# The first layer norm of a four-layer graph kernel: a fixed order on three engines, a centring product kept in PSUM, and the listing of pairs cut into pieces

## The chip, the cores and the metric

The kernel runs on one core of a Trainium2 chip. The metric is the device time of one execution in microseconds. The kernel before took 2083.43 us, the median of three runs (2079.95 to 2089.01). One more execution was profiled; it took 2082.92 us.

## The reference

Eight graphs of 2048 nodes with 64 features go through four layers. Each layer is a pre-norm residual block, and they share one adjacency matrix:

```python
h = jnp.maximum(_layernorm(x, axis=-1), 0.0)
x = x + layer(h)      # four different graph layers
```

with

```python
def _layernorm(x, axis=-1, eps=1e-5):
    m = jnp.mean(x, axis=axis, keepdims=True)
    v = jnp.var(x, axis=axis, keepdims=True)
    return (x - m) / jnp.sqrt(v + eps)
```

The first layer computes `industry`, the row-normalised adjacency matrix times `h @ W_ind`, and an attention between nodes and 64 hyperedges, whose membership matrix `H` (2048 x 64, zeros and ones) is given. Only the norm ahead of the first layer, the product with `W_ind` and the preparation of `H` are touched here.

## The kernel before, in words

The features lie transposed, two graphs on the 128 partitions: `xT[p]` is a block of 128 x 2048 for each of four pairs of graphs. The first norm treats each block in two halves of 1024 columns, so there are eight halves.

For one half the steps are: load `x` in two DMAs of 128 x 512; multiply it on TensorE by `avg`, a matrix that holds 1/64 in each graph's 64 x 64 block, which leaves the mean in PSUM (`mean`, L744); subtract on DVE (VectorE) into `xc` in SBUF (L745); square on ACT (ScalarE, L746); multiply by `avg` again (`var`, L751); logarithm and exponential on ACT to get the reciprocal root (L752, L753); one DVE instruction for `max(xc, 0) * q` into `hn` (L754). Then eight products of 128 x 128 with `W_ind` give `py` (L902), in two PSUM tiles of four products each. ACT copies each `py` rounded into `Y[0]` (L904), and DVE writes the rounding difference into `Y[1]` (L905). After that comes the industry stage: for each of four columns of 512 nodes, 16 tiles of the adjacency matrix are streamed in eight transfers `at` (L932, issued by POOL into a ring of six buffers), and products `acc` (L940) sum both parts of `Y` over them. Between these products lie the members' units (`ph`, L982, and the ACT and DVE work behind it), and DVE sums the `at` tiles into `ds` (L945).

The listing of pairs, `pairs`, runs after the first block: it loads `M` and `MT` (the membership matrix and its transpose), turns them to zeros and ones on DVE (L846, L848), ranks the pairs by products with a triangular matrix (`pr`, L857, and `pc`, L861) and copies, adds and multiplies on DVE until `Q` is there (L868). It also reduces `MT` into a flag (`bad`, L878). The weights of layers 0, 1 and 2 are prepared after the second and third block, with small products `pw`, `pwc` and `pwb` on TensorE and many small DMAs on SP.

In this stage a scheduler orders the instructions of each engine when the program is built; it works from its own estimates of when each operand is ready. Some instructions are instead kept in the order of the text: those issued through `kit.mm` while `kit.strict` is on, and those issued through the wrapper `InOrder`. In the first norm of the kernel before, none but the loading of ACT's table are.

[...] The stage's tiles take them all: `mean` two, `var` two of two banks each, and a tag `yy` with two tiles of one bank, which `py`, `pr`, `pc` and the weights' small products take in turn. A tile is used again when its last reader is done.

Of the kernel before, what the change touches and what calls it, by code (L numbers as in the profile page):

```python
# [8 lines left out]
FP = mybir.dt.float32  # L9
FR = mybir.dt.float32r  # L10
AF = mybir.ActivationFunctionType
OP = mybir.AluOpType
# [622 lines left out]
class Kit:  # L635


    def __init__(self, tc, t, pool):
# [8 lines left out]
        for b2 in range(2):  # L647
            nc.vector.memset(self.avg[half(b2), half(b2)], 1.0 / F)
        self.eps = pool.tile([P, 1], FP, name="eps_f")
# [107 lines left out]
    def norm(self, *tiles):  # L757
        for _ in self.norm_steps(*tiles):
            pass


def layer0(kit, hn, x1_dram, open_early, late_tile, between):
# [40 lines left out]
    with ExitStack() as sA:  # L803
# [29 lines left out]
        def pairs(pool, ps):  # L833
# [4 lines left out]
            nc.vector.tensor_copy(slot, tmp)  # L838
            tri = pool.tile([P, P], FP, name="tri")
            nc.gpsimd.iota(tmp[:, 0:P], pattern=[[1, P]], base=0, channel_multiplier=-1)  # L840
            nc.vector.tensor_copy(tri, tmp[:, 0:P])
            nc.vector.tensor_scalar(tri, tri, 0.0, None, op0=OP.is_ge)
            for h in range(2):
                nc.sync.dma_start(out=M[:, :, h, :], in_=t["L0_gnn_H"].rearrange("(t p) e -> p t e", p=P))
            Mf = M.rearrange("p t h e -> p (t h e)")
            nc.vector.tensor_scalar(Mf, Mf, 0.0, None, op0=OP.is_gt)  # L846
            nc.sync.dma_start(out=MT, in_=t["HT"])
            nc.vector.tensor_scalar(MT, MT, 0.0, None, op0=OP.is_gt)  # L848
# [3 lines left out]
            past = pool.tile([P, NT], FP, name="past")  # L852
            for g in range(2):
                pr = ps.tile([P, 8, E], FP, tag="yy", name="pr")
                for k in range(8):
                    i = 8 * g + k
                    mm(pr[:, k, :], MT[:, i * P : (i + 1) * P], tri[0:E, 0:E], start=True, stop=True)  # L857
                nc.vector.tensor_copy(rank[:, 8 * g : 8 * g + 8, :], pr)
            nc.vector.tensor_copy(deg, rank[:, :, E - 1])
            pc = ps.tile([P, NT], FP, tag="yy", name="pc")  # L860
            mm(pc, tri, deg, start=True, stop=True)  # L861
            nc.vector.tensor_copy(past, pc)
            nc.vector.tensor_sub(first, past, deg)

            nc.vector.tensor_tensor(rank, rank, first[:, :, None].to_broadcast([P, NT, E]), op=OP.add)
            nc.vector.tensor_tensor(rank, rank, M[:, :, 0, :], op=OP.mult)
            for h in range(2):
                nc.vector.tensor_scalar(Q[:, :, h, :], rank, -1.0, None, op0=OP.add)  # L868
            nc.vector.tensor_tensor(mid, first, past, op=OP.add)
            nc.vector.tensor_scalar(mid, mid, -0.5, 0.5, op0=OP.mult, op1=OP.add)  # L870
            nc.vector.tensor_scalar(width, deg, 0.5, None, op0=OP.mult)

            lo = pool.tile([P, NT], FP, name="bad_t")
            nc.vector.tensor_reduce(bad[:, 0:1], deg, AX.X, OP.min)
            nc.vector.tensor_scalar(bad[:, 0:1], bad[:, 0:1], 0.5, None, op0=OP.is_lt)
            nc.vector.tensor_scalar(lo, past, SLOTS + 0.5, None, op0=OP.is_gt)
            nc.vector.tensor_reduce(bad[:, 1:2], lo, AX.X, OP.max)
            nc.vector.tensor_reduce(bad[0:E, 2:3], MT, AX.X, OP.max)  # L878
            nc.vector.tensor_scalar(bad[0:E, 2:3], bad[0:E, 2:3], 0.5, None, op0=OP.is_lt)


        with ExitStack() as s1:
            pool = s1.enter_context(tc.tile_pool(name="rank", bufs=1, reuse_waits="tile"))
            sb = s1.enter_context(tc.tile_pool(name="nf_sb", bufs=2, reuse_waits="tile"))
            ps = s1.enter_context(tc.tile_pool(name="nf_ps", bufs=2, space=PSUM, reuse_waits="tile"))
            kit.use_ln_exp()
            for p in range(NP):
                for hf in range(2):
                    s = cols(hf, HN)
                    x = sb.tile([P, HN], FP, tag="x", name="x", bufs=3)  # L890
                    for k in range(2):
                        nc.sync.dma_start(out=x[:, cols(k)], in_=t["xT"][p, :, cols(2 * hf + k)])
                    mean = ps.tile([P, HN], FP, tag="mean", name="mean", bufs=1)
                    var = ps.tile([P, HN], FP, tag="var", name="var")
                    xc = sb.tile([P, HN], FP, tag="xc", name="xc")
                    q = sb.tile([P, HN], FP, tag="q", name="q")
                    kit.norm(hn[p][:, s], x, mean, var, xc, q)
                    for c in (2 * hf, 2 * hf + 1):
                        py = ps.tile([P, 4, P], FP, tag="yy", name="py")
                        for k in range(4):  # L900
                            m = 4 * c + k
                            mm(py[:, k, :], hn[p][:, m * P : (m + 1) * P], W_ind, start=True, stop=True)  # L902
                        yh = Y[0][:, 4 * c : 4 * c + 4, p, :]
                        nc.scalar.copy(yh, py)  # L904
                        nc.vector.tensor_tensor(Y[1][:, 4 * c : 4 * c + 4, p, :], py, yh.bitcast(FP), op=OP.subtract)  # L905
                if p == 0:
                    pairs(pool, ps)
                if p == 1:
                    weights(pool, ps)
                    kit.layer1_weights(pool, ps)  # L910
# [1079 lines left out]
```

## Time and profile before

| what | value |
|---|---|
| median of three runs | 2083.43 us |
| the profiled execution | 2082.92 us |
| its span, first to last instruction | 2081.0 us |
| busy share of TensorE, DVE, ACT, POOL | 96%, 58%, 22%, 13% |
| first product of the first norm | 4.03 us from the start of the span |
| first `acc` product of the industry stage | 68.99 us |
| first `acc` product of its second column | 111.64 us |

The first norm with the listing and the weights is therefore a stretch of some 65 us out of 2081. In the profile, PE is TensorE's products and PEld its weight loads; a float32 product has two records. A row of the timeline gives the start, the duration, the engine and line, the operation, the tiles written and read, how many records were merged, and in brackets how long the engine sat idle before it and what ended that. A group's row gives busy time and the mean of one in ns, then the idle time before. Durations of TensorE overlap their neighbours', so the distance between two starts is what one costs.

### The profile page before, as it was taken

To read this page: it belongs to the slowest core of one execution; us is meant where nothing else is said; L and a number is where in the kernel's file an instruction comes from. 1 tells how busy PE (TensorE), PEld (TensorE's weight loads), DVE (VectorE), ACT (ScalarE), POOL (GpSimd) and SP (SyncE) were. 2 spreads that over 40 slices of the span, in tenths; PEclk is the share of its full clock that TensorE was granted. 3 is DMA by queue.
4 is the path that set the end of the run, shared out by engine and by line. 5 is a ranking of instruction groups with operands and counts; after the bars stand their busy time and mean duration, and the time that the engine had idled before them with its cause. 6 is when DMAs were issued, how large, how long until landed. Compare 5 with 4: busy or idle time off the path is not lost.

```text
span 2081.0 us, 23594 instructions
## 1 busy us (share of the span) xinstructions
PE 2005.6 (96%) x9164; PEld 1154.1 (55%) x9164; DVE 1196.8 (58%) x1882; ACT 455.5 (22%) x859; POOL 264.2 (13%) x383
## 2 busy tenths in 40 slices
PE   7999899887999999999999999999999999999997
PEld 4777655533322222227775557765477755577653
DVE  6667478976888888883224653225632156522355
ACT  4321244457112121112121111211111211112100
POOL 0211054422000000000001210002100012100022
PEclk9999899999999999999999999999999999999999
DMA  6666272157111111213200012101022000121000
GB/s 180 195 193 190 67 239 80 43 154 162 46 42 35 49 33 23 60 31 89 66 31 21 25 37 60 58 7 35 18 64 61 26 22 25 37 75 46 8 14 12
DMA packets 84251, 138.16 MB, mean 66 GB/s; under 512 B 32753, under 2 KB 33009, under 8 KB 81457
## 3 DMA queue, kind: packets, MB, share of 16 engines
q1 hardware_dynamic: 65200, 83.86, 13.7%
q0 software_dynamic: 18928, 52.70, 10.2%
q8 instruction: 74, 1.21, 0.2%
q14 instruction: 49, 0.39, 0.1%
HBM read 102.64 MB, written 37.03 MB: 67 GB/s over the span
## 4 chain that ended last, share of the span: by engine, by line
PE 68%; issue 15%; DVE 6%; POOL 4%; DMA 3%; ACT 2%; SPq 0%; POOLq 0%; DVEq 0%; ACTq 0%
PE acc L726 27%; PE o L726 11%; PE u L726 6%; PE dn L726 5%; PE acc L940 3%; PE pgs L1169 2%; PE var L726 2%; PE mean L726 2%; PE py L726 2%; POOL fold L1878 1%; DVE ex L1167 1%; DMA at<-in_adjT 1%; PE ph L726 1%; POOL ot L1879 1%; DMA iv<-ind_dram 1%
## 5 line engine op out<-in xcount | busy, mean ns | idle before, releaser
L726 PE MATMUL acc<-aT,parts 128*128 128x512 f32 x1664 | 456.0, 420 | 0.0
L726 PEld LDWEIGHTS acc<-aT,parts 128*128 128x128 f32 x1664 | 307.8, 188 | 111.8 <-issue 49.4
L1866 DVE TENSOR_TENSOR pr<-u,embf 128x512 f32<-128x512 f32 x256 | 170.7, 688 | 138.8 <-PE u L726 131.9
L1485 DVE SCALAR_TENSOR_TENSOR pt<-R,wd,aT 128x1024 f32<-128x1024 f32 x192 | 236.5, 1279 | 20.4 <-PE dn L726 6.6
L726 PE MATMUL u<-W3f,y 64*128 64x512 f32 x1024 | 241.0, 589 | 0.0
L726 PE MATMUL o<-pt,hS 128*64 128x512 f32 x1024 | 236.4, 599 | 3.0 <-DVE pt L1485 3.0
L726 PEld LDWEIGHTS u<-W3f,y 64*128 64x128 f32 x1024 | 99.2, 187 | 120.6 <-issue 120.6
L726 PEld LDWEIGHTS o<-pt,hS 128*64 128x64 f32 x1024 | 68.0, 136 | 161.4 <-issue 149.9
L940 PE MATMUL acc<-at,Y 128*128 128x512 f32 x512 | 137.0, 413 | 2.4 <-DVE ev L949 2.4
L726 PE MATMUL u<-W3f,v 64*128 64x512 f32 x512 | 138.8, 619 | 0.0
L726 PE MATMUL dn<-pt,vd 128*32 128x512 f32 x1024 | 123.1, 598 | 0.0
L1702 DVE TENSOR_TENSOR yb<-py,cb_f 128x512 f32<-128x512 f32 x32 | 22.1, 691 | 173.7 <-PE py L726 173.7
L1878 POOL TENSOR_TENSOR fold<-fold 128x256 f32<-128x256 f32 x64 | 47.7, 745 | 548.4 <-DVE fold L1877 510.6
L940 PEld LDWEIGHTS acc<-at,Y 128*128 128x128 f32 x512 | 95.8, 195 | 25.7 <-issue 4.3
L726 PE MATMUL acc<-aTl,parts 128*128 128x512 f32 x384 | 103.2, 405 | 0.0
L1870 DVE TENSOR_TENSOR pr<-pr 128x512 f32<-128x512 f32 x128 | 88.1, 688 | 2.2
L1485 DVE SCALAR_TENSOR_TENSOR pt<-R,wd,aTl 128x1024 f32<-128x1024 f32 x64 | 79.8, 1282 | 11.4 <-PE dn L726 8.2
L726 PEld LDWEIGHTS acc<-aTl,parts 128*128 128x128 f32 x384 | 72.2, 188 | 21.5 <-issue 5.7
L1169 PE MATMUL pgs<-mix,S 128*128 128x512 f32 x128 | 69.8, 635 | 13.1 <-POOL mix L1168 12.4
L1852 ACT COPY xs<-px 128x128 f32<-128x128 f32 x64 | 17.1, 267 | 272.7 <-POOL ot L1880 210.3
L1168 POOL TENSOR_TENSOR mix<-ex,wt 128x512 f32<-128x512 f32 x64 | 66.7, 1042 | 76.7 <-DVE ex L1167 66.4
L1770 POOL TENSOR_TENSOR bq<-bq,xp 128x512 f32<-128x512 f32 x16 | 20.5, 1283 | 434.1 <-DVE xp L1768 395.5
(321 smaller groups left out, 2672.8 us busy)
## 6 DMA issues: line engine op xcount, KB each, us to landing
at<-in_adjT POOLq DMA_DIRECT2D x32, 512.0 KB, 4.6
raw<-in_adjT SPq DMA_DIRECT2D x64, 256.0 KB, 3.4
aT<-in_adjT POOLq DMA_DIRECT2D x12, 1024.0 KB, 6.1
xp<-xd SPq DMA_DIRECT2D x45, 256.0 KB, 3.2
R<-r_dram SPq DMA_DIRECT2D x14, 512.0 KB, 3.8
hi_dram<-hi SPq DMA_DIRECT2D x16, 264.0 KB, 2.4
lo_dram<-lo SPq DMA_DIRECT2D x16, 264.0 KB, 3.4
hhi<-hi_dram POOLq DMA_DIRECT2D x16, 264.0 KB, 3.0
```

The lines of the kernel that those rows point to most:

```text
L726: one = self.nc.tensor.matmul(*args, **kw)
L940: mm(acc[p], Y[h][:, m, p, :], at[:, k, :], start=m + h == 0, stop=m == NT - 1 and h == 1)
L1167: nc.vector.scalar_tensor_tensor(ex, mix, 1.0, ex, op0=OP.max, op1=OP.min)
L1168: nc.gpsimd.tensor_tensor(mix, ex, wt[:, k, :, None].to_broadcast([P, B, F]), op=OP.mult)
L1169: return lambda: mm(flat(pg), S[:, k, :], flat(mix), start=k == 0, stop=k == NB - 1)
L1485: nc.vector.scalar_tensor_tensor(pt, R[b2], wd[:, m, b2 : b2 + 1], aT[m][:, s].bitcast(FP), op0=OP.max, op1=OP.mult)
L1702: nc.vector.tensor_tensor(yb, py, bias[:, None, :].to_broadcast([P, 4, P]), op=OP.add)
L1770: nc.gpsimd.tensor_add(bq, bq, xp)
L1866: nc.vector.tensor_tensor(a, u[h], emb[:, i, 8 * w : 8 * w + 8, None].to_broadcast([P, 8, F]), op=OP.mult)
L1870: nc.vector.tensor_add(pr[h], pr[h], a)
L1878: nc.gpsimd.tensor_add(fold[:, :, 0:2, :], fold[:, :, 0:2, :], fold[:, :, 2:4, :])
L1879: nc.gpsimd.tensor_add(ot, fold[:, :, 0, :], fold[:, :, 1, :])
```

## The change

`Kit` gets a matrix `cen`, the identity less `avg`. One product with it leaves `x - mean` in PSUM, where `xc` now stays: the square and the last DVE step read it there, and the subtraction L745 and the SBUF tile are gone. PSUM is dealt out anew: `xc` has two tiles of two banks, `var` has one.

The stage becomes a loop of ten steps over eight halves. In step i the text issues: the loads of half i+2; the variance and scaling of half i-1; the centring and squaring of half i; a piece of the listing; the products with `W_ind` of half i-2 and their two copies. The products go through `kit.mm` with `strict` on, and the ACT and DVE instructions through `InOrder`, so all three engines keep this order. `pairs` is a generator with a `yield` between pieces, and its DVE instructions go through the same wrapper; `MT` is now loaded ahead of `M`, and `M` is compared with zero in a later piece. The weights of layers 0, 1 and 2 are prepared in steps 3, 4 and 5; of these only the issuing place moves.

```diff
+        self.cen = pool.tile([P, P], FP, name="cen_f")
+        nc.vector.tensor_sub(self.cen, self.ident, self.avg)
...
-        def pairs(pool, ps):
+        def pairs(pool, ps, V):
...
+            nc.sync.dma_start(out=MT, in_=t["HT"])
+            for h in range(2):
+                nc.sync.dma_start(out=M[:, :, h, :], in_=t["L0_gnn_H"].rearrange("(t p) e -> p t e", p=P))
+            yield
+            V.tensor_scalar(MT, MT, 0.0, None, op0=OP.is_gt)
+            yield
             for g in range(2):
                 pr = ps.tile([P, 8, E], FP, tag="yy", name="pr")
                 for k in range(8):
                     i = 8 * g + k
-                    mm(pr[:, k, :], MT[:, i * P : (i + 1) * P], tri[0:E, 0:E], start=True, stop=True)
-                nc.vector.tensor_copy(rank[:, 8 * g : 8 * g + 8, :], pr)
-            nc.vector.tensor_copy(deg, rank[:, :, E - 1])
+                    kit.mm(pr[:, k, :], MT[:, i * P : (i + 1) * P], tri[0:E, 0:E], start=True, stop=True)
+                V.tensor_copy(rank[:, 8 * g : 8 * g + 8, :], pr)
+                if g:
+                    V.tensor_copy(deg, rank[:, :, E - 1])
+                yield
             pc = ps.tile([P, NT], FP, tag="yy", name="pc")
+            kit.mm(pc, tri, deg, start=True, stop=True)
+            V.tensor_copy(past, pc)
+            V.tensor_sub(first, past, deg)
+            V.tensor_tensor(rank, rank, first[:, :, None].to_broadcast([P, NT, E]), op=OP.add)
+            yield
+            Mf = M.rearrange("p t h e -> p (t h e)")
+            V.tensor_scalar(Mf, Mf, 0.0, None, op0=OP.is_gt)
+            V.tensor_tensor(rank, rank, M[:, :, 0, :], op=OP.mult)
+            yield
             for h in range(2):
-                nc.vector.tensor_scalar(Q[:, :, h, :], rank, -1.0, None, op0=OP.add)
+                V.tensor_scalar(Q[:, :, h, :], rank, -1.0, None, op0=OP.add)
+            yield
...
+            V.tensor_reduce(bad[:, 1:2], lo, AX.X, OP.max)
+            yield
+            V.tensor_reduce(bad[0:E, 2:3], MT, AX.X, OP.max)
+            V.tensor_scalar(bad[0:E, 2:3], bad[0:E, 2:3], 0.5, None, op0=OP.is_lt)
+            yield
...
-                    kit.norm(hn[p][:, s], x, mean, var, xc, q)
...
+            V, A = InOrder(tc, nc.vector), InOrder(tc, nc.scalar)
...
+            def centred(i):
+                x = xs.pop(i)
+                xc = xcs[i] = ps.tile([P, HN], FP, tag="xc", name="xc")
+                for k in range(2):
+                    kit.mm(xc[:, cols(k)], kit.cen, x[:, cols(k)], start=True, stop=True)
+
+            def squared(i):
+                q = qs[i] = sb.tile([P, HN], FP, tag="q", name="q")
+                A.activation(q, xcs[i], AF.Square)
+
+            def scaled(i):
+                p, hf = halves[i]
+                q = qs.pop(i)
+                var = ps.tile([P, HN], FP, tag="var", name="var", bufs=1)
+                for k in range(2):
+                    kit.mm(var[:, cols(k)], kit.avg, q[:, cols(k)], start=True, stop=True)
+                A.activation(q, var, AF.Ln, bias=kit.eps)
+                A.activation(q, q, AF.Exp, scale=-0.5)
+                V.scalar_tensor_tensor(hn[p][:, cols(hf, HN)], xcs.pop(i), 0.0, q, op0=OP.max, op1=OP.mult)
+
+            def mapped(i):
+                p, hf = halves[i]
+                pys[i] = []
+                for c in (2 * hf, 2 * hf + 1):
+                    py = ps.tile([P, 4, P], FP, tag="yy", name="py")
...
+            def halved(i):
+                p, hf = halves[i]
+                for c, py in pys[i]:
+                    A.copy(Y[0][:, 4 * c : 4 * c + 4, p, :], py)
+                for c, py in pys.pop(i):
+                    ms = slice(4 * c, 4 * c + 4)
+                    V.tensor_tensor(Y[1][:, ms, p, :], py, Y[0][:, ms, p, :].bitcast(FP), op=OP.subtract)
+
+            listed = pairs(pool, ps, V)
+            fetched(0)
+            fetched(1)
+            kit.strict = True
+            for i in range(len(halves) + 2):
+                if i + 2 < len(halves):
+                    fetched(i + 2)
+                if 0 < i <= len(halves):
+                    scaled(i - 1)
+                if i < len(halves):
+                    centred(i)
+                    squared(i)
+                next(listed, None)
+                if i > 1:
+                    mapped(i - 2)
+                    halved(i - 2)
+                if i == 3:
                     weights(pool, ps)
+                if i == 4:
                     kit.layer1_weights(pool, ps)
+                if i == 5:
                     kit.layer2_weights(pool, ps)
+            kit.strict = False
```

## The prediction

> **What bounds the kernel now.** I read the page first (engines, then the chain that ended last), then busy time by stretches, TensorE's instructions in order of time in the first 120 us, the groups of the first norm by shape, and who waited for whom. The profiled execution took 2082.92 us, its span 2081.0; the median shown is 2083.43. A change in us is made against the first and added to the last.
>
> The engines, from the page's first part, and the chain, from its fourth:
>
> ```profile
> PE 2005.6 (96%) x9164; PEld 1154.1 (55%) x9164; DVE 1196.8 (58%) x1882; ACT 455.5 (22%) x859; POOL 264.2 (13%) x383
> ...
> PE 68%; issue 15%; DVE 6%; POOL 4%; DMA 3%; ACT 2%; SPq 0%; POOLq 0%; DVEq 0%; ACTq 0%
> ```
>
> TensorE carries the kernel. What the first norm costs is thus how late it lets the products after it begin. Busy time by stretches (length, then PE, PEld, DVE, ACT, POOL, clock, DMA share, GB/s):
>
> ```profile
> 53.00:68.99 15.99, 13.38 (x72) 9.00 (x71) 9.22 (x20) 10.80 (x14) 3.61 (x5) 1.00 0.48 142
> 68.99:111.64 42.65, 40.29 (x198) 32.13 (x196) 26.18 (x78) 8.88 (x35) 8.93 (x14) 1.00 0.74 211
> 111.64:150.00 38.36, 38.36 (x177) 30.84 (x178) 25.86 (x78) 7.27 (x31) 4.99 (x7) 0.96 0.60 183
> ```
>
> From 68.99, where the first acc product starts, TensorE is busy but for 2.4 us. So a us at 68.99 is a us at the end; from the second column on the build lays every engine's instructions in the same order as before. TensorE in order of time (start, duration; x16 is eight products, as float32 products have two records each):
>
> ```profile
> 4.03 3.75 PE L726 MATMUL mean<-x,avg_f 128*128 128x512 f32 x4 [4.03 <-DMA x<-in_xT]
> 9.10 3.78 PE L726 MATMUL mean<-x,avg_f 128*128 128x512 f32 x4 [1.31 <-DVE xc L745]
> 12.67 2.06 PE L726 MATMUL var<-q,avg_f 128*128 128x512 f32 x4
> ...
> 25.93 3.78 PE L857 MATMUL pr<-tri,MT 64*128 64x64 f32 x32 [1.33 <-DVE Y L905]
> 29.64 3.38 PE L726 MATMUL mean<-x,avg_f 128*128 128x512 f32 x4
> ...
> 50.63 1.95 PE L902 MATMUL py<-W_indf,hn 128*128 128x128 f32 x16
> 52.41 3.60 PE L726 MATMUL var<-q,avg_f 128*128 128x512 f32 x8
> 55.85 1.88 PE L726 MATMUL mean<-x,avg_f 128*128 128x512 f32 x4
> ...
> 67.19 2.05 PE L902 MATMUL py<-W_indf,hn 128*128 128x128 f32 x16 [1.33 <-DVE Y L905]
> 68.99 2.07 PE L940 MATMUL acc<-at,Y 128*128 128x512 f32 x8
> ```
>
> By starts: a product pass over a half (mean or var) takes 1.72 (52.41 to 55.85, two of them), cold 3.57 (9.10 to 12.67); py of a half 1.78 (50.63 to 52.41); all of pr 3.71. Warm work is 8 x (1.72 + 1.72 + 1.78) + 3.7 + 1.6 for pc and the weight products = 47.1 us of the 65.0 from 4.03 to 68.99; some 5 of the rest are three cold passes.
>
> DVE and ACT groups of this stage (busy, mean ns; idle before):
>
> ```profile
> L754 DVE SCALAR_TENSOR_TENSOR hn<-xc,q 128x1024 f32<-128x1024 f32 x8 | 9.8, 1223 | 5.4 <-ACT q L753 5.4
> L745 DVE TENSOR_TENSOR xc<-x,mean 128x1024 f32<-128x1024 f32 x8 | 9.7, 1218 | 8.5 <-PE mean L726 8.3
> L752 ACT ACTIVATE q<-var,eps_f 128x1024 f32<-128x1024 f32 x8 | 8.9, 1107 | 2.9 <-PE var L726 2.9
> L878 DVE TENSOR_REDUCE bad<-MT 64x1 f32<-64x2048 f32 x1 | 2.3, 2267 | 0.0
> ```
>
> **What the Trainium skill says.** "PSUM — Partial Sum Buffer", Engine vs sequencer instructions: ScalarE's and VectorE's queues are strict FIFO; so a DVE instruction that waits holds all behind it. The trace agrees: in the first column a ds (L945) sat 3.79 us on its transfer and the ev copies behind it came late. "VectorE: DVE Perf Modes", Why PSUM operands drop a tier: a PSUM operand caps float32 at 1x. Agrees: L745 with its mean in PSUM 1218 ns, L754 all in SBUF 1223; so xc in PSUM costs hn nothing. "TensorE: Matmul & The Clock Gate", What's actually happening: half rate until about 3.4 us of busy, and again after such an idle window. The passes of 3.75, 3.57 and 3.2 us agree in size, though the clock column shows 1.00 at the first two.
>
> **The change part by part.** The eight mean passes become eight passes by cen, equal at 1.72. Eight L745 go: 9.7 us of DVE, hidden under TensorE but for the step mean, xc, square. Square now reads PSUM: 0.05 more for each of eight (L752 from PSUM 1.11, L753 from SBUF 1.06), by as much less at the other end; I take 0.05, most of it hidden. cen adds a DVE subtraction (0.2) behind slot (0.4): first product 4.15 in place of 4.03. Moves on SP: x2 goes ahead of MT and M, MT ahead of M (issued about 5.5 and 7.4 to 11.3; MT is needed at 16.2, M at 44: hidden), x4 ahead of half of W0f, which may land at 20 to 21, while DVE has hn1 behind it at 20.0 (0 to 1, taken as 0), x7 ahead of b and b2c. POOL's first at waits for Q, now about 56 in place of 39.36; the rest go at 61 to 65, as before (60.87 to 65.8), so they are hidden until about 72.
>
> The order now forced: in step i TensorE does var(i-1), xc(i), a piece of the listing, py(i-2); DVE does hn(i-1), the piece, then the two Y differences of i-2. py, pr, pc and pw share two PSUM tiles, freed by those DVE instructions. So py or pw of a later moment stands behind hn(i-1) and a whole piece. From the end of var to hn's end takes 3.55 (52.41's first pass ends 54.3, its hn at 57.86); from there I add the listing's pieces by their rows (M > 0 1.23, rank products 1.22, rank copies 0.69, Q 1.29 both, Y difference 0.65 in a row). Square 1 ends at 15.9: first xc 4.15 to 7.85 cold, var0 9.0 to 12.6 cold, Ln, Exp, square in a row 3.2. The steps:
>
> ```
> step  PE from-to    hn done  DVE through  PE waits for
> 2     15.9-23.0     21.2     24.4         -
> 3     23.0-31.3     29.5     32.5         1.0, rank copy behind hn2
> 4     31.3-38.95    36.6     39.4         0.8 past, 1.1 Y difference (for pw1)
> 5     38.95-49.5    44.7     48.4         3.6 and 1.0 for pw of layer 2
> 6     49.5-54.7     54.75    57.3         -
> 7     54.7-59.95    60.0     62.2         -
> 8     59.95-63.45   65.2     69.1         -
> 9     68.5-70.3     -        73.1         5.0, py7 for Y differences of 6
> ```
>
> Step 3: hn2 is held to 28.3 by W1x's copy, which waits for W1f (SP issues it near 26, 2.0 to land). Step 5: py3 ends at 44.2; DVE has hn4 (43.0 at the earliest; 43.9 if b2r waits for b2c, issued near 40 and 3.3 to land; I take the middle), then M > 0 and rank times M, then the difference that frees the first pw's tile: 44.7 + 1.23 + 1.22 + 0.65 = 47.8 (47.3 to 48.2). Four pw through two tiles take another 1.2. Step 8: var7 runs 59.95 to 61.65, hn7 ends 3.55 later at 65.2, and the 2.27 us reduction of MT, with ones_r and bad (0.35), stands ahead of the differences of half 6. That is the costliest edit: work that had lain anywhere on an idle DVE now lies between hn7 and py7.
>
> So acc starts at 70.3, not 68.99: +1.3. Two idle gaps of 3 to 5 us can each cool the clock: 0 to 1.85 each; I take half, +1.8. In the first column ph needs the bank of the last py, whose difference is laid behind ds pairs: 73.1 in place of 72.2, then ph of the second member waits 0.2: +1.1 (from 0 if ACT is quicker to 2). Sum +4.2: 2082.92 + 4.2 = 2087.1, by the median 2087.6. The 2.4 us wait for ev at the end of the column stays: its at, ds and ev stand in the same order and start from TensorE's own progress. Of the 17.9 us that warm, gapless work would save (65.0 - 47.1), none is left.
>
> **The rivals.** *As meant:* no waits in the middle. Even then square 1 ends at 15.9, the warm products up to var7 take 36.7 (six var, six xc, pr, pc, six py, 1.35 of pw), var7 1.72, hn7 3.55, the reduction and differences 3.9, last py 0.9: acc at 62.65, -6.3, so 2077. For it: TensorE has 5.2 us a step and ACT only 4.4. Against it: the shared pair of tiles. It shows that faster by 0.5% (10.4 us, about what a measurement can tell from no change) is almost out of reach. *Cold clock, slower:* after step 5 the gaps keep TensorE at half rate through steps 6 to 9: three var, two xc and four py, 15.7 us warm. All cold (3.57 for 1.72) adds 17 to 2.4, my sum without the clock term: 2103; it passes 10.4 when over 7.4 us of that warm work run cold. For it: 29.64 is cold after only 1.33 us idle and small products. Against: the passes from 33 on are warm through idle of up to 1.3. *Late at, a transfer on the path:* DVE has five ds ahead of the first lo, so the fifth's landing gates ph. Before, five landed within 11 us of 65.8; if x1's DRAM copies and they meet, at5 lands at 80 in place of 75: +5 over mine, 2092. *The product doesn't replace the subtraction cheaply:* excluded by the rows above to 0.4 us.
>
> **How the numbers follow.** Forecast 0.72; as meant 0.12; cold 0.12; late at 0.04. The forecast's own range is +0 to +9. Faster 0.04 (as meant with scatter; three runs before spread 2080 to 2089), same 0.82, slower 0.14 (cold, and the forecast's tail). Range 2079.5 to 2096: it leaves out the far half of as meant and of cold.
>
> **What would show it.** Right: L745 gone; DVE's MT reduction directly ahead of two Y differences, with TensorE idle some 5 us before the last py; an idle of 3 to 4 before the first pw of layer 2; acc at 70 to 73; 111.64 answered by 114 to 117. Wrong: acc before 66 (tiles free earlier than I think), or after 76 (clock or transfers), or equal acc starts and unequal ends, which would put the cause beyond this stage.

## The result, and the profile after

The changed kernel took 2099.39 us, the median of seven runs (2094.82 to 2104.44); the kernel before took 2083.59 in the same comparison. The ratio is 1.0066, 95% interval 1.0046 to 1.0087: slower by 15.8 us, where +4.2 was forecast and the range ended at +12.6. The profiled execution took 2099.39 us, its span 2097.5, so 16.5 more than the span before.

Where in the span does it arise? The page of the changed kernel, its engines and its chain:

```profile
PE 2007.9 (96%) x9164; PEld 1155.2 (55%) x9164; DVE 1189.0 (57%) x1875; ACT 455.0 (22%) x859; POOL 264.5 (13%) x383
...
PE 66%; issue 16%; DVE 6%; POOL 5%; DMA 4%; ACT 2%; SPq 0%; POOLq 0%; DVEq 0%; ACTq 0%
```

TensorE is busy for only 2.3 us more than before (2007.9 us against 2005.6). Most of what was added is waiting, which the totals don't place. Busy time by stretches of the changed kernel, cut at the same events as before (first acc, first acc of the second column; columns: length, PE, PEld, DVE, ACT, POOL, clock, DMA share, GB/s):

```profile
53.00:80.15 27.15, 20.76 (x93) 14.56 (x93) 16.62 (x36) 11.81 (x15) 4.53 (x6) 0.86 0.53 156
80.15:127.94 47.79, 43.64 (x196) 33.92 (x195) 24.94 (x75) 8.93 (x35) 8.98 (x14) 0.94 0.63 174
```

The first acc starts at 80.15 in place of 68.99. The first column is longer too. As the event that ends it I take the `pd` product at the start of the second column, which lies beyond the wait for ev: 115.61 before, 130.59 after, so the column takes 50.44 us where it took 46.62. That is +11.2 and +3.8, together +15.0 of the 16.5. The places, in the waits of TensorE up to the first acc (engine and operation that waited, what it waited for, us in total, times, longest):

```profile
PE py L729 <- DVE rank L630: 4.9, 1, 4.9
PE py L729 <- DVE Y L630: 4.7, 1, 4.7
PE xc L729 <- DMA x<-in_xT: 4.3, 1, 4.3
PE pw L715 <- DVE Y L630: 3.1, 1, 3.1
```

The first product's 4.3 was there before (4.0). The 4.7 and the 3.1 are in the forecast (5.0 and 3.6). The 4.9 is not. TensorE around these waits in order of time. The variance product ahead of the wait takes 1.98 us and the one behind it 3.62, so it ran cold, at about half the rate; the last py and the first acc behind their wait are as cold:

```profile
14.30 1.98 PE L729 MATMUL var<-q,avg_f 128*128 128x512 f32 x4 [1.54 <-ACT q L630]
...
25.92 2.07 PE L729 MATMUL py<-W_indf,hn 128*128 128x128 f32 x8 [4.91 <-DVE rank L630]
27.79 3.62 PE L729 MATMUL var<-q,avg_f 128*128 128x512 f32 x4
...
76.72 3.78 PE L729 MATMUL py<-W_indf,hn 128*128 128x128 f32 x16 [4.74 <-DVE Y L630]
80.15 3.28 PE L996 MATMUL acc<-at,Y 128*128 128x512 f32 x8
```

Why is `rank` late? DVE of the changed kernel in order of time:

```profile
13.36 1.23 DVE L630 SCALAR_TENSOR_TENSOR hn<-xc,q 128x1024 f32<-128x1024 f32 x1 [8.66 <-ACT q L630]
15.90 1.22 DVE L630 TENSOR_SCALAR MT<-MT 64x2048 f32<-64x2048 f32 x1 [1.31 <-DMA MT<-in_HT]
23.91 0.23 DVE L827 COPY W0x<-W0f 128x128 f32<-128x128 f32 x1 [6.79 <-DMA W0f<-in_L_gnn_W]
24.05 1.22 DVE L630 SCALAR_TENSOR_TENSOR hn<-xc,q 128x1024 f32<-128x1024 f32 x1
25.19 0.68 DVE L630 COPY rank<-pr 128x512 f32<-128x512 f32 x1
```

A copy of 0.23 us that nobody needs before the first acc stands ahead of the second hn, and waits 6.79 us for W0f. That hn's own input had been ready at some 18.6, where its exponential ended on ACT:

```profile
17.52 1.06 ACT L630 ACTIVATE q<-q 128x1024 f32<-128x1024 f32 x1
```

Behind the hn came the rank copy, which frees the tile for the second half of py. W0f is late on SP (start, time on the queue):

```profile
5.28 0.47 SPq L847 DMA_DIRECT2D MT<-in_HT  x1
5.79 9.31 SPq L849 DMA_DIRECT2D M<-in_L_gnn_H  x2
15.23 2.68 SPq L904 DMA_DIRECT2D x<-in_xT  x2
18.01 0.47 SPq L684 DMA_DIRECT2D W0f<-in_L_gnn_W  x1
18.58 1.00 SPq L904 DMA_DIRECT2D x<-in_xT  x2
19.64 0.47 SPq L684 DMA_DIRECT2D W0f<-in_L_gnn_W  x1
```

and in the kernel before:

```profile
4.33 3.94 SPq L844 DMA_DIRECT2D M<-in_L_gnn_H  x2
...
12.28 1.11 SPq L681 DMA_DIRECT2D W0f<-in_L_gnn_W  x2
```

The two loads of M occupied SP for 3.94 us there and for 9.31 here; W0f's second half goes out 6 to 7 us later. In the first column POOL has its transfers in another order. The timeline of the changed kernel, of all engines, cut to this:

```profile
86.05 0.72 POOL L988 DMA_DIRECT2D at<-in_adjT  x1 [13.50 <-PE acc L996]
91.94 0.56 POOL L798 DMA_DIRECT2D hhi<-hi_dram  x1 [5.18 <-DMA hi_dram<-hi]
92.49 0.71 POOL L988 DMA_DIRECT2D at<-in_adjT  x1
...
99.68 1.23 DVE L1001 TENSOR_TENSOR ds<-ds,at 128x1024 fp32r<-128x1024 f32 x1 [5.43 <-DMA at<-in_adjT]
...
109.16 0.07 DVE L1031 MEMSET hi<- 128x8 f32 x1 [4.77 <-DMA hi_dram<-hi]
...
113.06 0.83 PE L1038 MATMUL ph<-W0x,hn 128*128 128x132 f32 x4 [2.50 <-DVE es L1046]
```

The eighth adjT tile stands behind hhi, a load that TensorE first reads at 261.2 us, after the four columns, and which waits 5.18 us for its own data in DRAM. The tile then takes 7.2 us from issue to landing. The sum ds waits on it for 5.43 us with the members' work behind it on DVE. So this unit's hi is stored late, DVE waits 4.77 us for that store before it may clear hi for a later unit, and ph, behind it, holds TensorE for 2.50. Before, the eighth tile went out first, and took 4.6 us to land:

```profile
78.25 0.71 POOL L932 DMA_DIRECT2D at<-in_adjT  x1 [3.87 <-PE acc L940]
79.19 0.56 POOL L799 DMA_DIRECT2D hhi<-hi_dram  x1 [0.23 <-issue]
```

There the eighth tile followed the seventh by 4.58 us. By that spacing it could have gone out at some 90.6 in the changed kernel, so that hhi held it for an estimated 1.9 us, and the slower landing added 2.6. Why the landing was slower is not shown; hhi and hlo go out on either side of it. By the rows of TensorE, the 3.8 us of the column are 2.5 of waiting for ph and some 1.5 and 1.2 for two groups of acc that ran cold, behind that wait and at the column's start, less some 2 at its end, where the wait for ev was shorter (1.65 for 2.36) and the products behind it warm.

### The profile page after: what moved, and what is told of

Same layout as the page of the kernel before. It is cut to its first block, busy times and chain, and to the rows that moved or that the text cites. A ratio compares the mean times of both kernels' runs of the same rounds, so it can differ in the third digit from the quotient of the medians.

```text
span 2097.5 us, 23590 instructions
## 1 busy us (share of the span) xinstructions
PE 2007.9 (96%) x9164; PEld 1155.2 (55%) x9164; DVE 1189.0 (57%) x1875; ACT 455.0 (22%) x859; POOL 264.5 (13%) x383
## 4 chain that ended last, share of the span: by engine, by line
PE 66%; issue 16%; DVE 6%; POOL 5%; DMA 4%; ACT 2%; SPq 0%; POOLq 0%; DVEq 0%; ACTq 0%
PE acc L729 27%; PE o L729 11%; PE u L729 6%; PE dn L729 5%; PE var L729 2%; PE py L729 2%; PE pgs L1225 2%; PE mean L729 2%; POOL fold L1934 1%; PE acc L996 1%; DVE ex L1223 1%; DMA iv<-ind_dram 1%; POOL ot L1935 1%; PE ph L729 1%; POOL mix L1224 1%
## 5 line engine op out<-in xcount | busy, mean ns | idle before, releaser
L1934 POOL TENSOR_TENSOR fold<-fold 128x256 f32<-128x256 f32 x64 | 47.8, 747 | 547.9 <-DVE fold L1933 510.0
```

The lines of the kernel that those rows point to most:

```text
L1934: nc.gpsimd.tensor_add(fold[:, :, 0:2, :], fold[:, :, 0:2, :], fold[:, :, 2:4, :])
```

## The experiments

Markers in one table: first acc, the `pd` of the second column, their distance (the first column), the median time, and the ratio to the kernel before with its interval. The medians are of 4 to 20 runs each. Profiled starts come from one execution each, whose own time can lie several us from the median (2098.4 against 2090.3 where DVE is left to the scheduler), and in which another product may run cold.

| kernel | first acc | pd | column | us | ratio |
|---|---|---|---|---|---|
| before | 68.99 | 115.61 | 46.6 | 2083.6 | |
| changed | 80.15 | 130.59 | 50.4 | 2099.4 | 1.0066 (1.0046 to 1.0087) |
| W0x copy later | 75.52 | 127.59 | 52.1 | 2097.4 | 1.0075 (1.005 to 1.01) |
| all weights later | 76.67 | 125.57 | 48.9 | 2092.9 | 1.0050 (1.0034 to 1.0066) |
| one load of M | 82.94 | 133.33 | 50.4 | 2102.5 | 1.0088 (1.0059 to 1.0116) |
| MT reduction early | 76.04 | 122.72 | 46.7 | 2090.7 | 1.0032 (1.002 to 1.0045) |
| product alone | 74.63 | 120.41 | 45.8 | 2090.3 | 1.0033 (1.0023 to 1.0043) |
| DVE left to the scheduler | 76.89 | 124.45 | 47.6 | 2090.3 | 1.0026 (1.0016 to 1.0036) |
| products at the start | 79.50 | 129.61 | 50.1 | 2095.6 | 1.0063 (1.0038 to 1.0087) |
| features' loads last | 79.45 | 124.37 | 44.9 | 2091.8 | 1.0034 (1.0024 to 1.0043) |
| the same, products at the end | 78.31 | 124.30 | 46.0 | 2093.5 | 1.0041 (1.0024 to 1.0059) |
| all mended | 62.48 | 109.83 | 47.4 | 2077.2 | 0.9970 (0.9958 to 0.9982) |
| all mended, no products at the start | 65.74 | 110.51 | 44.8 | 2079.4 | 0.9981 (0.9967 to 0.9994) |
| all mended and more | 61.95 | 105.92 | 44.0 | 2074.3 | 0.9948 (0.9931 to 0.9965) |

**The W0x copy alone.** Issued through the wrapper, it is laid behind the Avf instruction of the same function.

```diff
-            nc.vector.tensor_copy(Wx[:, 0:P], W)
+            V.tensor_copy(Wx[:, 0:P], W)
```

> One edit to the changed kernel: the copy W0x<-W0f no longer stands ahead of the second hn on VectorE, but behind the first half's Y differences. Theory A (VectorE's fixed order stands on late weight loads): the second hn starts at about 18.6 us instead of 24.05, but the next copy of the same kind, W1x<-W1f (landed 30.37), still stands ahead of the third hn, and b2r (its b2c landed 47.76) ahead of the fifth, so the chain is caught again: the third hn at about 30.6 (33.74 in the changed kernel), the fifth at about 48.2 (50.18). First acc about 2 us earlier than 80.15, time 2096 to 2098. Rival B (the hold is the 9.3 us of SP, whatever VectorE's order is, as x and MT come late too): second hn earlier, but first acc within 0.5 us of 80.15. Rival C (the one hold is the whole cost): first acc at 73.5 to 74, time 2093.

Measured: the second hn starts at 20.37. In this execution the first variance product ran cold (3.78 us where the changed kernel had 1.98), or it would have been 18.6. The third hn is caught by the next weights, as theory A says; DVE:

```profile
28.90 0.26 DVE L826 TENSOR_SCALAR Avf<-ones_f,avf 128x64 f32<-128x64 f32 x1 [3.89 <-DMA avf<-in_L_gnn_av]
29.07 0.22 DVE L630 COPY W0x<-W0f 128x128 f32<-128x128 f32 x1
29.97 0.23 DVE L697 COPY W1x<-W1f 128x128 f32<-128x128 f32 x1 [0.68 <-DMA W1f<-in_L_gnn_W]
30.11 1.22 DVE L630 SCALAR_TENSOR_TENSOR hn<-xc,q 128x1024 f32<-128x1024 f32 x1
```

The first acc comes 4.6 us earlier, more than the 2 expected, as b2c landed at 45.1 and not at 47.8. The column grew by 1.6 us, so the time shows only 2.0 less, which the runs' scatter does not separate from none. Rival B (no effect at acc) falls; so does C (this is the whole cost).

**All four late weights behind.** A method lays an instruction behind the last one of the wrapper:

```diff
+    def behind(self, name, *args, **kw):
+        one = getattr(self.engine, name)(*args, **kw)
+        self.tc.add_manual_dep(one.ins, self.last.ins.name, ...)
...
-            nc.vector.tensor_copy(Wx[:, 0:P], W)
+            V.behind("tensor_copy", Wx[:, 0:P], W)
```

and likewise for Avf, W1x and b2r.

> The changed kernel with all four VectorE instructions on late weights (W0x<-W0f, Avf<-avf, W1x<-W1f, b2r<-b2c) put behind the Y differences of their step, so that none stands ahead of an hn that does not need it; nothing else is edited. Theory A: second hn at about 18.6 (24.05), third at 26.5 to 27.5 (33.74), steps 2 and 3 end at 21 to 22 and 30.5 to 31.5 (27.79 and 37.91 in the changed kernel), first acc 6 to 7 us earlier than 80.15, at 73 to 74; time about 2093. Rival B (SP's late loads hold the chain elsewhere, on x or on the small weights that the products pw need): first acc 0 to 3 us earlier. Rival D (a fixed order of three engines costs this by itself): no more than 2 us.

Measured: hn starts at 20.27 and 27.61 (24.05 and 33.74), the first again behind a cold variance product; the fourth variance product starts at 31.66 (37.91). TensorE's 4.9 us wait is gone. But the fifth runs cold, though only waits of 0.9 us lie ahead:

```profile
39.63 3.64 PE L737 MATMUL var<-q,avg_f 128*128 128x512 f32 x4
```

From there it has nothing left on the W0x experiment (first pw of layer 2 at 49.87 and 49.73). First acc 3.5 earlier, not 6 to 7; the time, 6.5 less, is what A had. So the hold is real, and rival D falls (B, with 0 to 3 us, is missed by little); but cold products took back part of what its removal freed, and the waits of steps 5 and 9 stand untouched. With the hold gone, and the first variance product cold as forecast, steps 2 and 3 end at 23.40 and 31.66, where the prediction's own table has 23.0 and 31.3.

**One load of M.**

```diff
-            for h in range(2):
-                nc.sync.dma_start(out=M[:, :, h, :], in_=...)
+            nc.sync.dma_start(out=M[:, :, 0, :], in_=...)
+            nc.gpsimd.tensor_copy(M[:, :, 1, :], M[:, :, 0, :])
```

> The changed kernel with one of M's two loads from DRAM left out; GpSimd copies the first half of M into the second, so the values are the same. VectorE's order on W0f stays. Theory A (the root is the 9.31 us that SP spends issuing M's two loads): SP is free 4.65 us sooner, W0f lands at about 19.3 instead of 23.9, the hold falls from 6.8 us to 1 to 2 us, the product behind it stays warm (2.0 instead of 3.6 us); first acc 5 to 6.5 us earlier than 80.15, time about 2094. Rival B (the issue's length is waiting on descriptors that other loads would have waited on too): W0f lands less than 2 us sooner, and the first acc moves by less than 2 us.

Both were wrong on the first acc, though W0f landed at 19.35, as theory A had it. SP stood for nearly as long, on the next load (SP of this kernel):

```profile
5.79 0.59 SPq L848 DMA_DIRECT2D M<-in_L_gnn_H  x1
6.50 8.09 SPq L684 DMA_DIRECT2D W0f<-in_L_gnn_W  x1
```

so the 9.31 us are not the price of issuing M twice; on what SP stands there the records don't show, and it stays open. And the scheduler laid W0f's copy one place further ahead, before the first hn (DVE of this kernel):

```profile
19.35 0.23 DVE L827 COPY W0x<-W0f 128x128 f32<-128x128 f32 x1 [14.65 <-DMA W0f<-in_L_gnn_W]
19.50 1.22 DVE L630 SCALAR_TENSOR_TENSOR hn<-xc,q 128x1024 f32<-128x1024 f32 x1
```

W0f landed 4.6 us sooner, and the first acc came 2.8 us later. So the place of the copy decides, as much as the landing of its data.

**The reduction of MT early.** The two instructions move from the last piece to the first, behind `MT > 0`.

```diff
             V.tensor_scalar(MT, MT, 0.0, None, op0=OP.is_gt)
+            V.tensor_reduce(bad[0:E, 2:3], MT, AX.X, OP.max)
+            V.tensor_scalar(bad[0:E, 2:3], bad[0:E, 2:3], 0.5, None, op0=OP.is_lt)
```

> The changed kernel with the 2.27 us reduction of MT moved from between the last hn and the Y differences of half 6 to the step of MT>0, where VectorE waits for W0f. In the order built for it GpSimd and VectorE also go back to the order of before in the first column (the eighth adjT tile ahead of hhi). Theory A: the wait of 4.74 us before the last py falls to about 2.4, the product behind it is less cold (3.78 to between 2.0 and 3), first acc 2.5 to 4 us earlier than 80.15; and the first column, 3.8 us longer than before in the changed kernel, gives back about 2.7 of it. Time about 2093. Rival E (the first column is longer because the clock is cold, not because of the order): only 2.5 to 4 us in all, time 2096. Rival F (Y waits on ScalarE, not on the reduction): the first acc moves by less than 1 us.

TensorE of this kernel:

```profile
73.93 2.46 PE L729 MATMUL py<-W_indf,hn 128*128 128x128 f32 x16 [2.28 <-DVE Y L630]
76.04 3.38 PE L996 MATMUL acc<-at,Y 128*128 128x512 f32 x8
```

The wait fell from 4.74 to 2.28, the first acc by 4.1, and the column, in the old order, is 46.7 again, although its first products are cold (3.38). Rivals E and F fall. Time 8.7 less, of which about half each.

**The features' loads last**, the column's order by itself:

```diff
-        nc.gpsimd.dma_start(out=hi, in_=hi_dram[i].bitcast(FR))
-        nc.gpsimd.dma_start(out=lo, in_=lo_dram[i].bitcast(FR))
+        for o, d in ((hi, hi_dram), (lo, lo_dram)):
+            tc.keep_in_program_order(nc.gpsimd.dma_start(out=o, in_=d[i].bitcast(FR)))
```

> The changed kernel with the loads of the list features (hhi, hlo) put behind all 32 loads of the adjT tiles on GpSimd's queue; before the first acc nothing is edited. Theory A (the first column is longer than before because the eighth adjT tile stands behind hhi, which waits for hi_dram, and the sums ds behind that): first acc at 80.15 within 0.7 us, the first column (first acc to the pd of the second column's start) 46.8 to 47.5 us in place of 50.6, time 2095 to 2096. Rival E (the clock is cold at its start, 3.3 us for the first eight acc): the column 49 us or more. Rival: the features are now late for the sweep that follows near 440 us, and what is won is lost there.

Measured: column 44.9, which is 1.7 shorter even than before, with the wait for ev down to 1.18; time 7.5 less. Of the 5.5 us that the column lost, 1.1 is the first group of acc, which ran warm here (2.22 for 3.28); the rest goes with the features' loads among the adjT tiles, and nothing was lost at the sweep. All of these loads were moved; the exchange of the eighth tile and hhi was not tried by itself. In the experiment on the reduction, where POOL and DVE are back in the old order, the column is 46.7, and that is the better measure of what the new order cost: the +3.8. The other versions agree: where hhi goes ahead of the eighth tile the column takes 48.9 to 52.1 us (five kernels), where the tile goes first 44.8 to 47.6 (six), and with the features' loads last 44.0 to 46.0 (three). So the 1.7 below the kernel before lie within the spread of the old order.

**Products in the wait ahead of the last py**, on that kernel:

```diff
+                if i > len(halves):
+                    warm = ps.tile([P, HN], FP, tag="var", name="var", bufs=1)
+                    for k in range(4):
+                        kit.mm(warm[:, cols(k % 2)], kit.avg, hn[0][:, cols(k)], start=True, stop=True)
```

> The kernel with the features' loads behind the adjT tiles, and with four products more of the matrix of the mean with hn (two passes of 512 columns each, not read) in the wait ahead of the last py. Theory (a wait of some 5 us costs a second time, as the clock falls: 3.78 us for the last py in place of 2.05, 3.28 for the first eight acc in place of 2.1): both are quick, and the first acc's second group starts 2.5 to 3 us sooner than with the loads moved alone; time 2.5 to 3 us less. Rival (the clock is a matter of the time, not of the idle): both stay at 3.3 to 3.8 us; or the products added end late, and hold the last py back by up to 1 us.

The last py is warm (2.05 in place of 3.65), the first acc 1.1 us earlier, but pd stands at 124.30 against 124.37, and the time is not less (2093.5 and 2091.8). The expectation of 2.5 to 3 us is wrong: the cold pass at this place is hidden, as behind it TensorE waits for DVE's members' work (ph waits 1.57 for es in place of 0.40).

**Products at the start.**

```diff
+            warm = ps.tile([P, HN], FP, tag="var", name="var", bufs=1)
+            for k in range(5):
+                kit.mm(warm[:, cols(k % 2)][:, 0:P], kit.avg, kit.avg, start=True, stop=True)
```

> The changed kernel with five more products of the matrix of the mean with itself (128x128, their result is not read) ahead of the first product, at about 1.5 us, where TensorE waits for x and the centring matrix until 4.1 us. Theory (the clock is granted for earlier work): the first centring product takes 2 to 2.8 us in place of 3.6, the product of the variance behind it stays at 2.0; the second hn waits for W0f as before, so nothing of this reaches the first acc: 80.15 within 0.7 us, time as the changed kernel within 2 us. Rival: the clock stays low over the waits as well, both products 3.6 to 3.8 us.

The first centring product took 3.27 us, less than 3.59 but above the 2 to 2.8 expected (in the two mended kernels below that have the same five products, 3.77 and 3.04), the variance product 1.98; first acc 0.65 earlier. The four runs lie within the spread of the changed kernel's. Little to be had, as W0f holds the second hn anyway.

**The product alone**, in the kernel before, with the scheduler's order:

```diff
-                    xc = sb.tile([P, HN], FP, tag="xc", name="xc")
+                    xc = ps.tile([P, HN], FP, tag="xc", name="xc")
...
-                    kit.norm(hn[p][:, s], x, mean, var, xc, q)
+                    for k in range(2):
+                        mm(xc[:, cols(k)], kit.cen, x[:, cols(k)], start=True, stop=True)
...
```

> The kernel before with one part of the change alone: the centring product left in PSUM (in place of the product of the mean and the subtraction), in the order that the scheduler gives; listing and loads as before. If the product itself is good and the written order is what cost the time (theory A): 1 to 4 us faster than before, 2079 to 2082, first acc at 65 to 69 us (68.99 before). If reading PSUM on ScalarE and VectorE or the shared PSUM costs something (rival): slower than before, 2085 or more. If nothing bounds this stage but the listing: within 1 us of before.

Slower, which the expectation gave to PSUM reads. They are not it. The groups of the changed kernel (busy, mean ns; idle before):

```profile
L630 DVE SCALAR_TENSOR_TENSOR hn<-xc,q 128x1024 f32<-128x1024 f32 x8 | 9.8, 1224 | 25.6 <-ACT q L630 25.6
L630 ACT ACTIVATE q<-xc 128x1024 f32<-128x1024 f32 x8 | 8.1, 1008 | 6.0 <-PE xc L729 6.0
```

In the kernel with the product alone they took 1219 and 1019. From SBUF, in the kernel before, hn took 1223, and the square 1058:

```profile
L746 ACT ACTIVATE q<-xc 128x1024 f32<-128x1024 f32 x8 | 8.5, 1058 | 19.6 <-DVE xc L745 13.6 <-DVE first L863 5.9
```

It is again an order; DVE of the kernel with the product alone:

```profile
15.40 1.23 DVE L848 TENSOR_SCALAR M<-M 128x2048 f32<-128x2048 f32 x1 [10.70 <-DMA M<-in_L_gnn_H]
17.59 1.22 DVE L850 TENSOR_SCALAR MT<-MT 64x2048 f32<-64x2048 f32 x1 [0.97 <-DMA MT<-in_HT]
18.84 2.28 DVE L880 TENSOR_REDUCE bad<-MT 64x1 f32<-64x2048 f32 x1
21.05 1.21 DVE L905 SCALAR_TENSOR_TENSOR hn<-xc,q 128x1024 f32<-128x1024 f32 x1
```

The scheduler put 4.7 us of the listing, on late transfers, ahead of the first hn, which before had started at 17.35 with only `M > 0` ahead of it. TensorE waited 7.05 us for it. That the scheduler did so because it reckoned DVE free without the subtractions is likely, but was not tried. Nor was the other half of the rival, what it costs that `var` has one PSUM tile here where it had two.

**DVE left to the scheduler**, TensorE and ACT in the text's order:

```diff
-            V, A = InOrder(tc, nc.vector), InOrder(tc, nc.scalar)
+            V, A = nc.vector, InOrder(tc, nc.scalar)
```

> The changed kernel with VectorE's instructions of the first norm and of the listing left to the scheduler; TensorE and ScalarE keep the text's order. In the order built, the reduction of MT, M>0 and W0x<-W0f stand ahead of the second hn, the reduction and M>0 even ahead of the first. Theory A (what costs is an instruction on a late transfer ahead of an hn, by whomever it is placed): the first hn waits for M (it landed some 3 to 6 us behind 13.4), the second for W0f at 23.9 as in the changed kernel, so steps 2 to 4 are not quicker; but the last py no longer waits for the reduction (4.74 to about 2.4 us) and the 3.1 us of step 5 fall to about 2. First acc 75 to 77 us (80.15), the first column again 46.8 us, time 2090 to 2092. Rival D (the pinning itself costs): the second hn before 20 us, first acc at 70 us, time about 2085.

As theory A says: the first hn starts at 20.94 behind `M > 0`, the second at 23.51 behind the W0x copy; first acc 76.89, time 2090.3. So pinning DVE is not by itself what costs: the scheduler's order stands on the same loads. The 9 us less come with a last py that waits 2.43, as the reduction no longer stands ahead of it, and with a first column of 47.6. TensorE and ACT kept the text's order, so what pinning these costs was not tried.

**All mended.** The `behind` lines from above, and:

```diff
+                if i > 4:
+                    next(listed, None)
                 if 0 < i <= len(halves):
                     scaled(i - 1)
...
-                next(listed, None)
+                if i < 5:
+                    next(listed, None)
+                if i == 4:
+                    weights(pool, ps)
...
                 if i > 1:
                     mapped(i - 2)
                     halved(i - 2)
-                if i == 3:
-                    weights(pool, ps)
```

with layers 1 and 2 in the same way at steps 5 and 6, the four products of layer 2 in one tile, the reduction as a piece of its own ahead of `M > 0`, and the five products at the start.

> All repairs together on the changed kernel: the VectorE instructions on late weights behind the Y differences; the reduction of MT and M>0 in front of the scaling of a step, where VectorE is idle, in place of behind it; the products on weights one step later and ahead of py, the four of the second layer in one PSUM tile; five products more at the start, whose result is not read. Theory A: the 6.8 us hold, the 3.1 us of step 5 and 2.4 of the 4.7 us before the last py are gone, first acc at 66 to 69 us, the first column 46.8 us as before, time 2077 to 2083, within 0.3% of before or faster. Rival B (the loads on SP catch the chain wherever VectorE's order lets go): first acc at 72 us or later, time 2087 or more.

TensorE of this kernel at the end of the stage:

```profile
60.67 2.05 PE L735 MATMUL py<-W_indf,hn 128*128 128x128 f32 x16 [2.42 <-DVE Y L630]
62.48 2.09 PE L1008 MATMUL acc<-at,Y 128*128 128x512 f32 x8
```

17.7 us earlier than the changed kernel, 6.5 earlier than before, and faster than before by 0.3%. The rival that the loads on SP would catch the chain anyway falls.

> All repairs together, without the five products at the start. If these products matter only as far as the second product is warm: first acc at 62.5 to 64.5 us against 62.48 with them, time 2077 to 2079. Rival (the warm start carries the whole stage): first acc at 65 or later.

Without the five products the last py is cold (3.67) and the first acc at 65.74, as the rival had it and not 62.5 to 64.5; but at pd 0.7 us of that is left, and the intervals of the two times (2079.4 and 2077.2) overlap. That the five products made the difference is not shown: the first centring product took 3.75 us without them and 3.77 with them, and the two executions run within 0.04 us of each other until py behind the wait for b2r (1.77 and 1.78). TensorE from there, without the products and with them:

```profile
47.33 2.75 PE L735 MATMUL py<-W_indf,hn 128*128 128x128 f32 x16
49.87 2.98 PE L735 MATMUL var<-q,avg_f 128*128 128x512 f32 x4
...
47.36 2.14 PE L735 MATMUL py<-W_indf,hn 128*128 128x128 f32 x16
49.34 1.88 PE L735 MATMUL var<-q,avg_f 128*128 128x512 f32 x4
```

> All repairs together, and three more: the products on the second layer's weights a step later (the wait of 1.78 us for b2r goes), the last py in the PSUM of an xc that is free (its wait of 2.42 us falls by 0.6 us, to the scaling itself), and the features' loads behind the adjT tiles. First acc at 60 to 61 us against 62.48, the first column as before or 1 us shorter, time 2074 to 2076. Rival: the waits move on to the next thing late, time within 0.5 us of 2077.2.

First acc at 61.95; the wait for b2r stayed at 1.78 (it is laid behind an hn in the later step as well), the last py's fell to 1.83. The column is 44.0, and the time 2074.3: the best version, 0.5% faster than before. Against the kernel with all mended, the first acc is 0.5 us earlier and the column 3.4 shorter, so the features' loads are the likely source of the last gain; the three additions were not tried apart.

## Why the prediction was wrong, point by point

**The step that failed** is in the part on SP's moves: W0f "may land at 20 to 21, while DVE has hn1 behind it at 20.0 (0 to 1, taken as 0)". The mechanism was seen, that a copy of W0f stands ahead of hn1; its size was not. W0f landed at 23.9, and hn1, ready at 18.6 by then (the first variance product was warm, which the forecast had cold), started at 24.05: a hold of 5.4 us where nothing was taken. The slip is in SP: M's loads "7.4 to 11.3" took the 3.94 us that the kernel before showed for them, in another place of the queue; they took until 15.10. The same slip reached W1f, b2c and all that stands behind.

What it was worth, by the table of steps (end of the step on TensorE, forecast and measured):

| step | forecast | measured | off | what came in |
|---|---|---|---|---|
| 2 | 23.0 | 27.79 | +4.8 | hn1 held for W0f |
| 3 | 31.3 | 37.91 | +6.6 | the variance product behind that wait cold, 3.62 |
| 5 | 49.5 | 56.51 | +7.0 | 3.1 and the small waits as forecast |
| 6 | 54.7 | 62.90 | +8.2 | cold again behind 3.1 us, 3.05 |
| 8 | 63.45 | 71.72 | +8.3 | |
| acc | 70.3 | 80.15 | +9.9 | last py cold, 3.78 |

Of the 9.9 the clock term had 1.8, so acc missed by 8.1: 4.8 by the hold, and most of the rest by the clock, as below. That the hold is the step that failed, and not the arithmetic around it, is seen with all weights later, where steps 2 and 3 end within 0.4 us of the forecast. The second miss is the first column: +1.1 forecast, +3.8 measured. The forecast held that the order ahead of the ev wait would stay and looked for the delay in the bank of the last py. That delay did not come (the first ph, at 83.27, does not wait); the order of POOL was not the same in that column, and with the old order back it takes 46.7. 4.2 + 8.1 + 2.7 is 15.0, what pd shows.

**What held.** The reduction between the last hn and the differences of half 6: 5.0 forecast, 4.74 measured, and 2.28 with the reduction moved. The first pw of layer 2: 3.6 and 3.1. The product's price: no loss; the square was forecast 0.05 us dearer from PSUM and was 0.05 cheaper. "A us at 68.99 is a us at the end" held for the second column's pd to within some 2 us in all versions: 15.0 there is 15.8 in the time, for the mended kernels -5.8 is -6.4 and -9.7 is -9.8. It did not hold for the first acc itself: products in the last wait brought it 1.1 us forward and nothing at pd.

**The clock term** was right in kind and too small. By starts, three passes ahead of acc took 3.41, 2.89 and 3.43 us for 1.72, 1.72 and 1.78: 4.5 us in all, where the forecast had 1.8. One of them stands behind the hold that it had not priced. The Trainium skill, "TensorE: Matmul & The Clock Gate", What's actually happening, says that the activity window runs freely, so the same kernel may count differently many cold products from run to run. The runs agree: the same first variance product, after the same 1.11 us wait, took 1.98 or 3.53 to 3.78 in different versions. An idle of 3.4 us, as the prediction had it, was not needed: with all weights later a pass took 3.64 us behind waits of 0.9 at most, and behind the same wait of 1.8 us the next pass was warm in one of the two mended kernels shown above and cold in the other. A cold pass costs some 1.7 us only where no later wait hides it: at the start the hold for W0f hid it, at the end DVE did.

**The rivals.** *As meant* had the first acc at 62.65 and 2077 for a stage without waits in the middle; the mended kernel gives 62.48 and 2077.2. That the two meet to 0.2 us is in part luck: square 1 ended 1.7 us sooner than in the sum, as the first variance product ran warm; the middle took 40.4 us and not 36.7, with 2.3 of waits; and var7 to acc took 7.9 and not 10.1, as the reduction had been moved away. *Cold clock* at 2103 came nearer the measured time than the forecast, but for another reason: steps 7 and 8 ran warm. *Late at* named the right resource, an adjT tile on POOL late in the first column, but the eighth and not the fifth. Its cause, a meeting with other transfers, may be half of it: the tile was issued late, behind hhi, which the rival did not have, and then took 7.2 us to land where it had taken 4.6.

## What to carry to other kernels

An engine that takes its instructions in order makes each of them as late as the latest transfer ahead of it: before fixing or trusting an order, list every instruction ahead of the critical one that reads a fresh load, and price its landing in the new queue order, not by its duration in the old one. Put such copies, and work that can wait, behind the critical instruction of the step; a fixed order holds only what is pinned, and the pieces that a scheduler still places move with every edit, far behind the edit too. Read the gain at an event that lies past the next wait, since a product that starts sooner may only wait there.

## What the runs showed that I had not expected

- Two loads of M in rows of 256 bytes kept SP for 9.31 us in one place of its queue and for 3.94 in another. With one of them left out, the next load, a 64 x 64 block, stood for 8.09 us.
- With a load that is first read 169 us later one place ahead on POOL's queue, the first column took 3.8 us more than in the old order; with all such loads laid last it took 44.0 to 46.0 us in three kernels, where the old order took 44.8 to 47.6 in six.
- ScalarE's square took 1008 ns from PSUM and 1058 from SBUF; VectorE's hn 1224 and 1223.
- Taking one subtraction of 1.2 us a half off VectorE, by the product in PSUM alone, made the kernel slower by 0.33%: the scheduler's order of the rest changed with it.
- Two executions of the mended kernels ran within 0.04 us of each other for 47 us, and then one product took 1.88 us in one and 2.98 in the other.
